# Flamingo block (two cross-attentions, two feed-forwards) on one core: the read-back of the probabilities, four orders behind other instructions, and the start of the projections

## The chip, the cores and the metric
One core of a Trainium2 chip. The metric is the device time of one execution in microseconds (us), as the median of several runs. Engines are named as the profile names them: PE (matmul), PEld (its weight loads), DVE (VectorE), ACT (ScalarE), POOL (GpSimd), SP (SyncE, which here only issues DMAs; its queue is "SPq").

## What is computed
Eight rows of 128 tokens, width 512, pass four steps, each added to the running `x` with a tanh gate. The first cross-attention has 32 heads of 128 and fills most of the time:

```
x = x + tanh(g_xattn[0]) * L0_xattn(layernorm(x), ctx)   # 32 heads, position bias, masked softmax
x = x + tanh(g_ffn[0])   * L0_ffn(layernorm(x))          # 4-bit weights, 512 -> 512
x = x + tanh(g_xattn[1]) * L1_xattn(layernorm(x), ctx)   # one head of width 512
x = x + tanh(g_ffn[1])   * L1_ffn(layernorm(x))          # base layer, router, 8 low-rank experts

# L0_xattn:  q = rms(x) @ w_q.T ; k = ctx @ w_k.T ; v = ctx @ w_v.T
#            p = softmax(mask(q k^T + position_bias)) ; out = x + (p v) @ w_out.T
```

## The kernel before
Every f32 product is made of three matmuls (L175 to L177): an operand is split into a high part (an fp32r cast on ACT, L166) and a low part (the difference, on DVE or POOL, L167), and high x high, high x low and low x high are added in PSUM. A 128x512 matmul follows its predecessor by about 0.227 us when nothing is late.

**Projections (0 to about 330 us).** `keys_and_queries` walks a list of 32 entries: 14 key pairs (a pair is two heads), 16 query pairs, the last 2 key pairs. The first two (`project_plainly`) use plain blocks: the inner halves in the outer loop, the four results copied by ACT (L552) after all matmuls. From the third on, `seven` uses seven half-size products P1 to P7 in the order P1, P5, P6, P2, P7, P4, P3. It has two PSUM accumulators that are read in between: `c1` is copied by ACT after P1 (L240), P6 (L247), P7 (L256) and P4 (L262), and the next product may add to it only after that copy; `c3` takes P5, is added by DVE to the copy of P7 (L257), and only then takes P3, after which DVE adds once more (L266). L251 adds P2. P4 and P3 of one entry run among the products of the next, so an iteration is some 9.5 us. Its weights are loaded two entries ahead (`load_pair`, L279); `sums_of` (L297 to L299, DVE) makes the sums of the entry after next at the end of each iteration, and `pair_parts` splits the parts in the next. The right operands come from the context (`context_operands`: eight blocks `cxB` split first, then four differences by DVE, L458, and their splits `cxT`) and from the rows of x (`query_operands`: for each of four steps two rows are normalised by `normed`, transposed by PE and split). `residual` (L577 to L583) scales rows of x, at entries 14, 16, 18 and 20. `early` is a generator of some 28 steps that prepares later weights (a load, a cast on ACT, a difference on POOL or DVE, two stores to DRAM; the last steps unpack the 4-bit weights: L841, L850, L851); it is pulled once or twice per entry from entry 13 on.

**Units (about 330 to 790 us).** 64 units, each one head for four rows. `unit(u)`: project_out of an earlier pair, some value products (`make_values`), `attend(u-4)`, `add_masks` (POOL, L633), `scores`: PE (L645), DVE adds the mask (L646) and takes the maximum (L650), DVE transposes the probabilities of u-3 (L691), ACT exponentiates (L660), DVE makes the factors (L665, L666), POOL multiplies (L668). `store_probs(u)` sends the tile to DRAM (L676); the loads for the next units are put behind that store on SP (L569 q and k, L363 bias, L279 weights); `move_probs(u)` reads it back in 32-row blocks with four DMAs (L683) into `moved`, of which there are two buffers. So the buffer that the read-back of u fills comes free when DVE has transposed u-2, which happens in unit u+1.

**End (about 790 us on).** `ending` interleaves the last units with the four-step tail (`ffn0`, `xattn1`, `ffn1`, a software pipeline over the eight rows; PE's order there and in the projections is fixed by `in_order`). The weights of the first feed-forward, `wf`, two DMAs of 1 MB, are issued ahead of it (L1031), as are four rows of biases (L1016); two of these are scaled by DVE (L1038, L1039).

**What sets the order.** Apart from the fixed orders on PE, the order of each engine's queue is settled when the program is built, by a list scheduler that goes by program order as priority and by its own estimate of durations. `behind(name)` adds an order only: on the engine of the marked instruction, what the block issues stands after it. Each queue then runs strictly in its order, so an instruction that waits holds up all behind it.

Of the kernel before, what the change touches and what calls it, by code (L numbers as in the profile page):

```python
# [14 lines left out]
ALU = mybir.AluOpType  # L15
# [48 lines left out]
def kernel(  # L64
# [55 lines left out]
    def wide_row(tag, name, dtype=F32):  # L120
        return slot([P, D], tag, name, dtype)
# [86 lines left out]
    def seven(name, left, right, kept, done, tokens=None):  # L208


        shape = [P, HALF * P] if tokens is None else [P, 2, N]

        def times(out, which, start, stop):
            w, t = left[which], right[RIGHT[which]]
            if tokens is None:
                terms = [
                    (
                        (w[:, 0, bass.ts(dc, P)], w[:, 1, bass.ts(dc, P)]),
                        (t[:, 0, dc, :], t[:, 1, dc, :]),
                    )  # L220
                    for dc in range(HK)
                ]
                product(out, terms, start, stop, skip_group_check=True)
                return
            for j in range(2):
                cols = bass.ts(2 * tokens + j, P)
                terms = [
                    (
                        (t[:, 0, dc, cols], t[:, 1, dc, cols]),
                        (w[:, 0, bass.ts(dc, N)], w[:, 1, bass.ts(dc, N)]),  # L230
                    )
                    for dc in range(HK)
                ]

                product(out[:, j, :], terms, start and j == 0, stop, skip_group_check=True)

        c1 = ptile(shape, "mm", f"c1_{name}")
        times(c1, "P1", True, False)
        c11 = kept(0, 0)
        mark("copy", nc.scalar.copy(c11, c1))  # L240
        yield
        c3 = ptile(shape, "av", f"c3_{name}")
        times(c3, "P5", True, False)
        yield
        times(c1, "P6", False, False)
        c12 = kept(0, 1)
        mark("copy", nc.scalar.copy(c12, c1))  # L247
        yield
        c2 = ptile(shape, "sc", f"c2_{name}")
        times(c2, "P2", True, True)  # L250
        mark("add", nc.vector.tensor_tensor(c11, c2, c11, ALU.add))  # L251
        done(0, 0, c11)
        yield
        times(c1, "P7", False, False)
        c22 = kept(1, 1)
        mark("copy", nc.scalar.copy(c22, c1))  # L256
        nc.vector.tensor_tensor(c22, c3, c22, ALU.add)  # L257
        done(1, 1, c22)
        yield
        times(c1, "P4", False, True)  # L260
        c21 = kept(1, 0)
        mark("copy", nc.scalar.copy(c21, c1))  # L262
        done(1, 0, c21)
        yield
        times(c3, "P3", False, True)
        nc.vector.tensor_tensor(c12, c3, c12, ALU.add)  # L266
        done(0, 1, c12)
        yield
# [147 lines left out]

    stats = keep([P, NB, 8], "stats")

    def normed(b):


        nc.vector.bn_stats(stats[:, b, 2:8], xs[b])
        nc.vector.bn_aggr(stats[:, b, 0:2], stats[:, b, 2:8])
        mean, var, r12 = (stats[:, b, i : i + 1] for i in range(3))
        nc.gpsimd.tensor_scalar(r12, var, 1.0 + 1e-5, 1e-10, ALU.mult, ALU.add)
        rsqrt(r12, r12)
        xq_b = wide_row("wo", f"xq_{b}")
        nc.vector.scalar_tensor_tensor(xq_b, xs[b], mean, lnw, ALU.subtract, ALU.mult)
        mark("xq", nc.scalar.activation(xq_b, xq_b, AF.Copy, scale=r12))
        return xq_b  # L430

    def right_pages(name):
# [2 lines left out]
    def context_operands():  # L435

        ops = right_pages("cx")
        ops["B12"] = page([P, 2, HK, HALF * P], "cxB12")
        blocks = {
            n: [cx_raw.pop((half, 2 * inner + i)) for i in range(HK)]  # L440
            for n, half, inner in (("B11", 0, 0), ("B12", 1, 0), ("B21", 0, 1), ("B22", 1, 1))
        }

        def put(n, i, src):
            o = ops[n]
            by_pool = i == 0 and n != "B11"
            split(o[:, 0, i, :], o[:, 1, i, :], src, nc.gpsimd if by_pool else nc.vector)

        for n, pair in blocks.items():
            for i, t in enumerate(pair):  # L450
                put(n, i, t)
        yield ops
        b11, b12, b21, b22 = blocks.values()
        for n, dst, one, two in (
            ("T1", b11, b12, b11), ("T2", b11, b22, b11), ("T3", b12, b22, b12), ("T4", b21, b21, b11)
        ):
            for i in range(HK):
                nc.vector.tensor_tensor(dst[i], one[i], two[i], ALU.subtract)  # L458
                put(n, i, dst[i])
        yield ops  # L460

    def query_operands():

        ops = right_pages("xq")
        for j in range(HALF):
            rows = [normed(j), normed(j + HALF)]
            blocks = []
# [37 lines left out]
            yield  # L507
            put("T3", t3)
            put("T4", t4)
            yield ops  # L510

    stored = {
# [19 lines left out]
    def project_plainly(kind, p, left, right):  # L532

        banks = {}
        for inner in range(2):
            for half in range(2):
                for i in range(2):
                    if inner == 0:
                        tag = ("mm", "av")[half]
                        banks[i, half] = ptile([P, HALF * P], tag, f"c{i}{half}_{kind[0]}{p}")  # L540
                    w, t = left[i], right[f"B{inner + 1}{half + 1}"]
                    terms = [
                        (
                            tuple(part[:, bass.ts(2 * inner + dc, P)] for part in w),
                            (t[:, 0, dc, :], t[:, 1, dc, :]),
                        )
                        for dc in range(HK)
                    ]
                    product(banks[i, half], terms, inner == 0, inner == 1)
        for (i, half), c in banks.items():  # L550
            t = slot([P, HALF * P], "kq", f"{kind}{i}{half}_{p}")
            mark("copy", nc.scalar.copy(t, c))  # L552
            nc.sync.dma_start(out=stored[kind, p][:, 2 * i + half], in_=t)

    fetched = {}

# [122 lines left out]
    def move_probs(u):  # L679
        moved = slot([P, NQ, HALF, Q32], "moved", f"moved_{u}")  # L680
        blocks = probs[u].rearrange("(i q) n f -> n q i f", q=Q32)
        for j in range(NQ):
            nc.sync.dma_start(  # L683
                out=moved[bass.ts(j, Q32)].rearrange("p i b k -> p i (b k)"), in_=blocks[j]
            )
        probs[u] = moved

    def transpose_probs(u):
# [199 lines left out]
    def keys_and_queries():  # L888
        nonlocal left, sums, before
        for n, (kind, p) in enumerate(order[:-1]):  # L890
# [24 lines left out]
                    else:  # L915
                        load_quad(0)
            before = now
            sums = sums_of(n + 2)
            if n == 3:
                with later():  # L920
                    prep_mask()
# [2 lines left out]
            if n in (14, 16, 18, 20):  # L924
                with later():
                    residual((n - 14) // 2)
            if n >= BEFORE - 1:
                for _ in range(2 - n % 2):
                    next(extra, None)
        for u in range(FIRST):  # L930
# [48 lines left out]
    def unit(u):  # L979
        p, r = divmod(u, 4)  # L980

        n = 2 * (u - OUT_LAG)

        goal = 14 + int(1.74 * (u - 3)) if u > 3 else 0
        if n >= 0:
            project_out(*divmod(n, NB))
        make_values((made + goal + 1) // 2)
        if u >= LAG:
            attend(u - LAG)
        if n >= 0:  # L990
            project_out(*divmod(n + 1, NB))
        make_values(goal)
        s = add_masks(u)
        for _ in range({0: 2, 1: 2, 2: 1, 3: 1, 4: 1}.get(u, 0)):
            next(last_keys)
        scores(u, s)
        store_probs(u)
        with behind("through"):
            loads(u + 1)
        move_probs(u)  # L1000
        if r in (2, 3):
            with behind("exp"):
                split_wo(2 * p + r - 2)
# [274 lines left out]
        nc.sync.dma_start(out=out[b], in_=o)  # L1278
        yield

    w_ffn = sum((load_page(f"wf{i}", ffn_kept[i]) for i in range(2)), [])
    wq1_p, bw, lora = [], {}, []
    rb = keep([P, NR], "rb")
    onehot = slot([P, NE * RANK], "bias", "onehot")[:NR]
# [24 lines left out]
    def ending():  # L1309

        outs = iter(range(2 * (NU - OUT_LAG), NP * NB))

        def project(n):
            for _ in range(n):
                project_out(*divmod(next(outs), NB))

        project(2)
        attend(NU - 4)
        with behind("x"):
            transpose_probs(NU - 3)  # L1320
        project(2)
        attend(NU - 3)
        project(1)
        yield
        project(3)
        with behind("x"):
            transpose_probs(NU - 2)
        make_values(14 * (H // 4 + 1) - 3)
        attend(NU - 2)
        yield  # L1330
        make_values(14 * (H // 4 + 1))
        transpose_probs(NU - 1)
        yield
        attend(NU - 1)
        project(4)
        yield
# [82 lines left out]
```

## Time and profile before

| | us |
|---|---|
| median of 3 runs (951.42 to 957.57) | 954.54 |
| the profiled execution, own time | 948.85 |
| its span, first to last instruction | 947.0 |
| PE busy / DVE / ACT / POOL | 918.2 / 667.2 / 504.9 / 468.2 |
| PE not busy over the span | 28.8 |
| of it in 0 to 24 / 24 to 56 / 155 to 310 | 4.4 / 3.9 / 5.7 |
| of it in 310 to 392 / 392 to 780 / 780 to 947 | 7.0 / 0.2 / 7.6 |

The profile numbers lines of the kernel (L257 is line 257). "PE x <- DVE y L257: 3.1, 2, 1.8" in the list of waits means that PE stood still before instructions on x until DVE's line 257 had written y: 3.1 us in all, 2 times, 1.8 us the longest. In the timeline a row gives start, duration, engine, line, operation and tiles, and in brackets the idle time before it and what ended that.

### The profile page before, as it was taken

The page shows a single profiled execution, that of the slowest core. Times are in us where ns is not written, and L with a number is a line of the kernel's source. Part 1 is how long each engine was busy: PE and PEld are TensorE (multiplying, and loading weights), DVE is VectorE, ACT ScalarE, POOL GpSimd, SP SyncE. Part 2 cuts the span into 40 slices and gives each one's busy share as a digit, 9 for nine tenths or more (in the row PEclk, how much of TensorE's full clock was granted, in tenths as well). Part 3 has the DMA queues.
Part 4 walks back from the last instruction along what each step waited for, and adds up shares of the span by engine and source line. Part 5 has one row for each costly group of instructions (what it writes and reads, how often), then busy time and mean ns, then how long its engine had stood idle before and what let it go on. Part 6 is the DMA issues. An engine that isn't in the chain of part 4 may idle for free.

```text
span 947.0 us, 16520 instructions
## 1 busy us (share of the span) xinstructions
PE 918.2 (97%) x5458; PEld 805.7 (85%) x5458; DVE 667.2 (70%) x1346; ACT 504.9 (53%) x1432; POOL 468.2 (49%) x516
## 2 busy tenths in 40 slices
PE   8999999999999989999999999999999999999998
PEld 6778888788877888899999999999999997888897
DVE  7787775677768786677667677667677676465686
ACT  5565654556564445454445545345454544487861
POOL 4744440113341365493865748476594852184441
PEclk9999999999999999999999999999999999999999
DMA  8545465698876946747676666868567556522001
GB/s 281 191 150 169 147 195 176 202 314 290 269 239 220 300 156 175 207 141 230 186 207 175 195 189 174 233 168 232 162 181 219 160 160 201 222 88 95 1 24 67
DMA packets 123908, 174.99 MB, mean 185 GB/s; under 512 B 16942, under 2 KB 52782, under 8 KB 122670
## 3 DMA queue, kind: packets, MB, share of 16 engines
q1 hardware_dynamic: 123822, 173.93, 60.5%
q8 instruction: 43, 0.70, 0.3%
q14 instruction: 43, 0.35, 0.1%
HBM read 109.85 MB, written 64.03 MB: 184 GB/s over the span
## 4 chain that ended last, share of the span: by engine, by line
PE 50%; DMA 3%; POOL 3%; ACT 3%; DVE 2%; issue 1%; SPq 1%; POOLq 0%; DVEq 0%; ACTq 0%
PE pso L175 6%; PE pso L177 6%; PE pso L176 6%; PE av L706 5%; PE c_v L175 5%; PE c_v L177 5%; PE c_v L176 5%; PE sc L645 5%; DMA k<-keys 1%; PE o L175 1%; DMA raw_wv<-in_wv_dram 1%; POOL cols L409 1%; PE o L177 1%; PE o L176 1%; ACT h L1068 1%
## 5 line engine op out<-in xcount | busy, mean ns | idle before, releaser
L660 ACT ACTIVATE s<-s,nm 128x128 f32<-128x128 f32 x256 | 99.8, 392 | 79.7 <-DVE nm L650 52.6
L725 DVE SCALAR_TENSOR_TENSOR x<-pso,tg,x 128x512 f32<-128x512 f32 x128 | 93.9, 742 | 34.0 <-PE pso L177 33.1
L175 PE MATMUL pso<-wo_h,a 128*128 128x512 f32 x256 | 106.0, 416 | 1.7 <-DVE x L725 1.7
L633 POOL TENSOR_TENSOR s<-mneg,bias 128x512 f32<-128x512 bf16 x64 | 75.7, 1190 | 59.7 <-DMA moved<-through 22.5
L668 POOL TENSOR_TENSOR s<-s,rs 128x512 f32<-128x512 f32 x64 | 66.7, 1041 | 69.1 <-DVE rs L666 51.3
L176 PE MATMUL pso<-wo_l,a 128*128 128x512 f32 x256 | 100.7, 395 | 0.0
L177 PE MATMUL pso<-wo_h,a 128*128 128x512 f32 x256 | 99.8, 399 | 0.0
L707 ACT CAST a<-av 128x512 fp32r<-128x512 f32 x64 | 37.3, 585 | 98.6 <-PE av L706 91.1
L175 PE MATMUL c_v<-wvP,cxT 128*128 128x256 f32 x288 | 84.2, 292 | 4.2 <-DVE keys L266 2.6
L176 PE MATMUL c_v<-wvP,cxT 128*128 128x256 f32 x288 | 82.9, 288 | 0.0
L177 PE MATMUL c_v<-wvP,cxT 128*128 128x256 f32 x288 | 82.3, 286 | 0.0
L706 PE MATMUL av<-pT,v 128*128 128x128 f32 x512 | 69.6, 277 | 0.0
L646 DVE TENSOR_TENSOR s<-sc,s 128x512 f32<-128x512 f32 x64 | 43.7, 685 | 34.3 <-POOL s L633 24.2
L645 PE MATMUL sc<-k,q 128*128 128x128 f32 x464 | 65.0, 275 | 1.6 <-DMA k<-keys 1.4
L706 PEld LDWEIGHTS av<-pT,v 128*128 128x128 f32 x512 | 65.2, 194 | 1.4
L645 PEld LDWEIGHTS sc<-k,q 128*128 128x128 f32 x464 | 60.8, 191 | 4.7 <-issue 1.9
L175 PE MATMUL c_v<-wvP,cxB 128*128 128x256 f32 x216 | 62.3, 288 | 2.1 <-DVE s L646 2.1
L708 DVE TENSOR_TENSOR a<-av,a 128x512 fp32r<-128x512 f32 x64 | 43.4, 679 | 28.9 <-ACT a L707 28.7
L177 PE MATMUL c_v<-wvP,cxB 128*128 128x256 f32 x216 | 61.9, 287 | 0.0
L175 PEld LDWEIGHTS c_v<-wvP,cxT 128*128 128x128 f32 x288 | 55.2, 192 | 7.8 <-DVE keys L266 2.8
L176 PE MATMUL c_v<-wvP,cxB 128*128 128x256 f32 x216 | 61.5, 285 | 0.0
L167 POOL TENSOR_TENSOR wvP<-raw_wv,wvP 128x512 fp32r<-128x512 f32 x41 | 53.6, 1317 | 7.8 <-ACT wvP L166 7.8
(280 smaller groups left out, 2809.7 us busy)
## 6 DMA issues: line engine op xcount, KB each, us to landing
keys<-keys SPq DMA_DIRECT2D x64, 256.0 KB, 3.1
queries<-queries SPq DMA_DIRECT2D x64, 256.0 KB, 3.8
through<-s SPq DMA_DIRECT2D x64, 256.0 KB, 2.5
moved<-through SPq DMA_DIRECT2D x256, 64.0 KB, 3.3
q<-queries SPq DMA_DIRECT2D x58, 256.0 KB, 4.2
k<-keys SPq DMA_DIRECT2D x58, 256.0 KB, 4.7
raw_wk<-in_wk_dram SPq DMA_DIRECT2D x32, 256.0 KB, 4.0
raw_wq<-in_wq_dram SPq DMA_DIRECT2D x32, 256.0 KB, 3.9
```

The lines of the kernel that those rows point to most:

```text
L167: mark("low", (low_engine or nc.vector).tensor_tensor(low, src, wide(high), ALU.subtract))
L175: nc.tensor.matmul(out, lhsT=lh, rhs=rh, start=first, stop=False, **more)
L176: nc.tensor.matmul(out, lhsT=lh, rhs=rl, start=False, stop=False, **more)
L177: nc.tensor.matmul(out, lhsT=ll, rhs=rh, start=False, stop=last, **more)
L633: nc.gpsimd.tensor_tensor(s, mneg[:, half], bias.unsqueeze(2).to_broadcast([P, NQ, HALF, Q32]), ALU.add)
L645: nc.tensor.matmul(ps[:, j, :], lhsT=q[:, cols], rhs=k[:, cols], start=True, stop=True)
L646: nc.vector.tensor_tensor(s, by_block(ps), s, ALU.add)
L660: e = nc.scalar.activation(one, one, AF.Exp, bias=nm[:, j : j + 1], accum_out=sm[:, j : j + 1])
L668: mark(f"norm{u}", nc.gpsimd.tensor_tensor(s, s, factors, ALU.mult))
L706: nc.tensor.matmul(av[:, b, :], lhsT=v[:, cols], rhs=pT[:, b, :], start=True, stop=True)
L708: mark("al", nc.vector.tensor_tensor(al, av, wide(ah), ALU.subtract))
L725: "x", nc.vector.scalar_tensor_tensor(xs[b], ps, factor, xs[b], ALU.mult, ALU.add, **out)
```

## The change
1. `sums_of` at the end of an iteration is put behind the DVE addition L257, which now carries the mark "add". (The mark also serves `later()`, so `residual`, `early` and the mask preparation stand behind L257 where they stood behind L251.)
2. `normed`: the statistics move to `row_stats`, called one step ahead, with one more small DVE instruction (minus mean times factor); the row is scaled first, by ACT out of x, and DVE multiplies by the weight after it. Before, DVE subtracted and multiplied and ACT scaled last.
3. `context_operands`: the low parts of the first eight blocks all go to DVE (three went to POOL); the differences and later low parts stand behind the last of them.
4. `project_plainly`: the second pair finishes one result after the other, and each result is copied and stored as soon as it is complete.
5. `early` starts at entry 11 and not 13.
6. `move_probs(u)` is issued in unit u+1, after the loads and behind the store of u+1 (the last two: before the last store, and at the start of `ending`).
7. The two loads of `wf` move into `ending`, behind the last read-back.

```diff
-        nc.vector.tensor_tensor(c22, c3, c22, ALU.add)
+        mark("add", nc.vector.tensor_tensor(c22, c3, c22, ALU.add))
...
+        nc.vector.scalar_tensor_tensor(
+            stats[:, b, 5:6], mean, -1.0, r12, ALU.mult, ALU.mult
+        )
+
+    def normed(b):
         xq_b = wide_row("wo", f"xq_{b}")
-        nc.vector.scalar_tensor_tensor(xq_b, xs[b], mean, lnw, ALU.subtract, ALU.mult)
-        mark("xq", nc.scalar.activation(xq_b, xq_b, AF.Copy, scale=r12))
+        nc.scalar.activation(
+            xq_b, xs[b], AF.Identity, bias=stats[:, b, 5:6], scale=stats[:, b, 2:3]
+        )
+        nc.vector.tensor_tensor(xq_b, xq_b, lnw, ALU.mult)
...
-        def put(n, i, src):
+        def put(n, i, src, engine=nc.vector):
             o = ops[n]
-            by_pool = i == 0 and n != "B11"
-            split(o[:, 0, i, :], o[:, 1, i, :], src, nc.gpsimd if by_pool else nc.vector)
+            nc.scalar.copy(o[:, 0, i, :], src)
+            mark(
+                "low",
+                engine.tensor_tensor(o[:, 1, i, :], src, wide(o[:, 0, i, :]), ALU.subtract),
+            )
...
+        marks["lows"] = marks["low"]
...
-                nc.vector.tensor_tensor(dst[i], one[i], two[i], ALU.subtract)
-                put(n, i, dst[i])
+                with behind("lows"):
+                    nc.vector.tensor_tensor(dst[i], one[i], two[i], ALU.subtract)
+                    put(n, i, dst[i], (nc.gpsimd, nc.vector)[i])
...
+        row_stats(0)
+        row_stats(HALF)
         for j in range(HALF):
             rows = [normed(j), normed(j + HALF)]
...
+            if j + 1 < HALF:
+                row_stats(j + 1)
+                row_stats(j + 1 + HALF)
             yield ops
...
+        turns = [(inner, half, i) for inner in range(2) for half in range(2) for i in range(2)]
+        if p:
+            turns.sort(key=lambda turn: (turn[1], turn[2], turn[0]))
+        for inner, half, i in turns:
...
+            product(banks[i, half], terms, inner == 0, inner == 1)
+            if inner:
+                t = slot([P, HALF * P], "kq", f"{kind}{i}{half}_{p}")
+                mark("copy", nc.scalar.copy(t, banks[i, half]))
+                nc.sync.dma_start(out=stored[kind, p][:, 2 * i + half], in_=t)
...
-            sums = sums_of(n + 2)
+            with behind("add"):
+                sums = sums_of(n + 2)
...
-            if n >= BEFORE - 1:
+            if n >= BEFORE - 3:
                 for _ in range(2 - n % 2):
                     next(extra, None)
...
         scores(u, s)
+        if u == NU - 1:
+            move_probs(u - 1)
         store_probs(u)
         with behind("through"):
             loads(u + 1)
-        move_probs(u)
+            if 0 < u < NU - 1:
+                move_probs(u - 1)
...
-    w_ffn = sum((load_page(f"wf{i}", ffn_kept[i]) for i in range(2)), [])
+    w_ffn = []
...
+        move_probs(NU - 1)
+        with behind("moved"):
+            for i in range(2):
+                w_ffn.extend(load_page(f"wf{i}", ffn_kept[i]))
         project(2)
         attend(NU - 4)
```

## The prediction
> **What bounds the kernel now.** The page comes first: which engine is full. Then a table of windows (time, busy time per engine, granted clock, DMA share, GB/s) shows where PE is not.
>
> ```profile
> PE 918.2 (97%) x5458; PEld 805.7 (85%) x5458; DVE 667.2 (70%) x1346; ACT 504.9 (53%) x1432; POOL 468.2 (49%) x516
> ```
> ```profile
> 24.00:56.00 32.00, 28.12 (x125) 22.04 (x124) 26.39 (x64) 19.85 (x50) 23.71 (x36) 1.00 0.49 159
> ...
> 310.00:345.00 35.00, 31.48 (x180) 27.83 (x179) 27.17 (x40) 14.99 (x37) 16.73 (x12) 0.95 0.79 267
> ...
> 392.00:780.00 388.00, 387.85 (x2681) 358.14 (x2680) 273.16 (x478) 187.44 (x617) 252.87 (x218) 1.00 0.67 188
> ```
> PE bounds it. From 392 to 780 us it never stands still, so nothing can be won there and much lost. The 28.8 us in which PE is not busy lie in the projections, the entry into the units and the end; whoever shortens no wait of PE there gains nothing. So next the list of what PE waited for (total, times, longest):
>
> ```profile
> PE c_q L175 <- DVE queries L257: 3.1, 2, 1.8
> PE c_q L175 <- ACT queries L240: 2.6, 2, 1.6
> PE c_v L175 <- DVE keys L266: 2.6, 1, 2.6
> PE c_v L175 <- DVE s L646: 2.1, 1, 2.1
> PE c_k L176 <- DVE cxB L167: 1.7, 3, 1.3
> PE c_k L175 <- ACT keys L247: 1.7, 1, 1.7
> PE pso L175 <- DVE x L725: 1.7, 3, 1.0
> PE c_k L175 <- ACT keys L240: 1.6, 1, 1.6
> PE sc L645 <- DMA k<-keys: 1.4, 1, 1.4
> ```
> These are single events, and for each the timelines of DVE and ACT show the instruction in front of the late one. Two of DVE's rows:
>
> ```profile
> 274.22 0.43 DVE L297 TENSOR_TENSOR more_wq<-raw_wq 128x256 f32<-128x256 f32 x1 [3.37 <-DMA raw_wq<-in_wq_dram]
> ...
> 275.36 0.68 DVE L257 TENSOR_TENSOR queries<-c_q,queries 128x512 f32<-128x512 f32 x1
> ```
> L257's input was ready: ACT ended the copy L256 at 269.9. It stood behind a sum that waited 3.37 us for a weight.
>
> Around a wait more is lost than is listed: at 36.64 the first matmul lasts 0.50 us and not 0.39, and the next follows after 0.33 and not 0.23, some 0.2 to 0.3 us each time. And the granted clock is 0.95 and 0.96 in the windows from 310 and 345, which is 0.05 x 35 = 1.75 us and 0.04 x 47 = 1.9 us; each drop stands right behind a wait of over 2 us (DVE keys, DVE s).
>
> **The change part by part** (us of the profiled execution; gains negative)
>
> *Sums behind L257.* In front of the two P3 that waited 3.1, L257 can go at 271 and 293: all of it, -3.1. The sums wait for the same load as before, one instruction later (0.6); behind them stand low parts that PE needs an iteration later. At 166 and 187 PE waited 2.6 for copy L240: ACT had two residual rows in front (L583, 1.5 us), which waited for DVE's L581, which stood among the sums waiting for a load until 163.04. L581 now comes after L257 and the sums, at some 164.1, while L240's input is there at 162.8 (1.36 after L256, as at 63.42 and 64.78), so the scheduler should put the copy first. Of 2.6 I take -2.0; if it keeps the residual first, 0.
>
> *Plain pair finished one by one.* At 36.64 PE waited 1.6 for L240, behind four copies L552 issued from 31.52 to 35.51 with casts among them. Now three lie before 29. -1.6. The same matmuls and DMAs are issued. The low part that held PE 0.5 at 33.84 stood in the same jam: -0.3.
>
> *Rows scaled first.* The 1.7 for L247 at 52.21: ACT stood at L429 waiting for two DVE multiplications that took 2.06 together while POOL worked. ACT's first step now needs only statistics made long before. But DVE now waits for ACT ahead of its multiplication (0.68), and its additions stand behind that: -1.2 of 1.7. Eight more small DVE instructions (0.16, row L580) have cover in DVE's idle time, 32 less 26.4; uncovered, 1.3.
>
> *First low parts on DVE.* Three low parts leave POOL, where they took 5.12 together from 9.10, and cost DVE 3 x 0.69. PE's two waits there, 0.34 (POOL) and 1.27 (DVE, late at 11.30 behind two differences that took 2.39) go: -1.6. The differences start some 3 us later, but their products are only needed at 32.7. The earlier waits, 5.0 to 9.2, are for loads and stay. [...]
>
> *`early` two entries sooner.* Its work moves about 19 us forward (two iterations of 9.5); per step a load, a cast (0.62), a low part (POOL 1.3 to 1.5, DVE 0.69) and two stores of 0.4 on SP. At 330.97 two L841 took 2.96 on DVE, and L850 and a score addition stood in front of L266, for which PE waited 2.6; then 0.6 and 0.3 on ACT's list. These go, -3.2, with the clock drop behind them, -1.75. Entries 11 and 12 take three steps more: ACT is 55.89 of 99 busy in the window from 56 to 155, and that is the cover; if a store is late, loads queue behind it, and sums, now out of L257's way, are late.
>
> *Read-back a unit later.* 256 DMAs of 0.43 us on SP move behind a store and two to four loads of 0.43. SP loses its two waits there (54 for the store to land, 33 for the transposition), which held up the next store by up to 3.7; as PE waits for none of this between 392 and 780, that is worth 0 there. At the entry I take -1.6 of the 3.5 for L646 and for k, and a quarter of the second clock drop, -0.45: the bias load that made the first late (issued 365.56, 5.57 us) keeps its place behind the store. The price: the list for `moved` gives
>
> ```profile
> DMA to landing us min/median/max: 1.8/3.3/6.1
> ```
> Taking the times of before, I put each read-back of u behind the store and loads of unit u+1, added three issues and 3.4 us, and compared with the transposition of u. The slack falls from a median of 7.4 (least 0.5) to 2.0; 13 of 62 come late, 17.5 us in all, on DVE. Two rows say what that costs PE: at 388.86 DVE stood 1.99 for a read-back and PE lost nothing; at 791.56 it stood 3.29 and PE lost 0.47. So 0 to 17.5 x 0.47 / 3.29 = 2.5; I take 1.1, as most are under 2.
>
> *`wf` loads behind the last read-back.* Two DMAs of 1 MB move from 786 to some 800; they landed in 8.4 and are first used at 817: 8 us of cover. The bias row that held DVE 3.29 shared the queues with them. -0.8 of the 1.7 for L725.
>
> *Waits that take their place.* Every queue is sorted anew. Between nothing and a wait for each one removed, I put two of the mean size in the list, 2.0: +4.0.
>
> Sum: 3.1 + 2.0 + 1.6 + 0.3 + 1.2 + 1.6 + 3.2 + 1.75 + 1.6 + 0.45 + 0.8 = 17.6; the restarts of some ten waits at 0.2 add 2.0: 19.6 gained. Given back 1.1 + 4.0 = 5.1. Net -14.5: 948.85 - 14.5 = 934.35 for such an execution. It lay 5.7 under the median of the runs, which I keep: 954.54 - 14.5 = 940.0.
>
> The clock by the page's rule (the Trainium skill, TensorE: Matmul & The Clock Gate, HAM clock gate): half rate after a whole idle window of about 3.4 us. Here waits of 2.6 and 2.1 were enough, while three of 1.6 to 1.7 before 56 us were not. If by the rule these drops had another cause and stayed, the net would be 14.5 - 2.2 = 12.3.
>
> **The rivals**
>
> *Given back at the entry* (0.28). The projections win, but the re-sorted entry and end keep waits as large as before: 3.2 + 1.75 + 1.6 + 0.45 + 0.8 = 7.8 fall away, net -6.7 or, with one more wait, -4.7: about 949. For it: those waits come from ACT, POOL and DMA together, and POOL idles 5.2 us for a load that doesn't move. Against: DVE's and POOL's `early` work is visibly in front.
>
> *The read-back too late: slower* (0.12). If it lands not in 3.4 but in 6.1 us, as it now queues behind q, k and weights of 256 KB, 41 of 62 come late, 82 us on DVE. DVE runs in order, and the x additions that free PE's banks stand behind. It decides from about a quarter of that on PE: 0.25 x 82 = 20.5 eats the 19.6. Half of it gives -14.5 + 41 = 26.5, or 981; a third, 967. For it: a slack of 2.0. Against: DVE is idle 115 of 388 us, and 1.99 cost nothing.
>
> *The change does not do what it says* (0.05). The scheduler had statistics and sums early already and moves them as before: 954 or so.
>
> *As summed* (0.55): 940, own range 930 to 946.
>
> **How the numbers follow.** A measurement of this kernel tells about 1%, 9.5 us, from no change: faster ends at 945. Of the likeliest, 0.48 of 0.55 lies under 945; of the rival at 949, 0.08. Faster 0.57 (with a little for more than I count). Slower takes the late read-back, 0.12 and 0.01; the rest, 0.30, is the same. The range goes from 929, nothing given back and the untaken rest of each part too (0.6 for L240, 0.5 for L247, 1.9 for L646 and k, 1.4 of clock, 0.9 for L725: 19.6 + 5.3 = 24.9), to 957, a read-back that eats the gain; the slower rival beyond is left out.
>
> **What would show it.** Right: no PE wait for L257, for keys L240 or L247, for cxB beyond 10 us; DVE's L297 after L257; the granted clock 1.00 from 310 to 392; SP without waits at L683. Wrong: DVE idle before L691 with "DMA moved" of over 40 us; PE waits between 392 and 780; the residual still ahead of L240; a clock drop elsewhere.

## The result and the profile after

The changed kernel took 942.62 us (median of 4 runs, 938.8 to 943.57) beside 952.98 for the kernel before (951.3 to 957.57): ratio 0.9876, 95% interval 0.9829 to 0.9923. Once more on another chip, where the kernel before took 948.41, it was 937.96 (experiment e9): ratio 0.9891 (0.9873 to 0.9910). By the medians both are 10.4 us faster; by the ratio the first is 11.8, with an interval from 7.3 to 16.3. The forecast was 14.5. The two executions with a profile differ less: span 947.0 before, 941.4 after, because the one of before lay under its median and the one of after did not.

The windows of the kernel after (columns: window, its length, busy us of PE, PEld, DVE, ACT and POOL with instruction counts, granted clock, DMA share, GB/s):

```profile
24.00:56.00 32.00, 28.73 (x127) 22.53 (x126) 29.67 (x70) 21.85 (x52) 24.08 (x37) 1.00 0.54 165
310.00:345.00 35.00, 33.51 (x227) 30.68 (x226) 25.32 (x43) 18.39 (x46) 11.51 (x10) 1.00 0.58 203
345.00:392.00 47.00, 41.22 (x287) 37.74 (x286) 27.23 (x51) 21.74 (x77) 24.86 (x22) 0.98 0.69 191
392.00:780.00 388.00, 385.65 (x2641) 355.49 (x2641) 268.94 (x477) 187.52 (x621) 251.63 (x216) 0.99 0.69 186
```

From 310 to 345 us the clock is 1.00 and PE is busy 2.0 us more than before. From 24 to 56 it is busy 0.6 more, and DVE is now busy 29.67 of 32. From 392 to 780 PE stands still for 2.35 us, where it was 0.15 before; all of it is one wait at 774.95. From 345 to 392 it stands still for 5.8 us, before for 3.5.

Its list of what PE waited for (total, times, longest):

```profile
PE av L726 <- DVE pT L711: 3.7, 3, 2.5
PE sc L664 <- DMA k<-keys: 2.3, 1, 2.3
PE c_k L177 <- DVE wkP L167: 1.9, 2, 1.1
PE c_q L175 <- ACT queries L247: 1.6, 3, 0.5
PE c_v L175 <- ACT wvP L166: 1.5, 1, 1.5
PE c_v L175 <- DVE s L665: 1.4, 1, 1.4
```

(Lines have moved: the transposition L691 is L711, the score addition L646 is L665, the score matmul L645 is L664, the read-back L683 is L702, the residual L583 is L602.) The waits for L257, L266, queries L240 and x L725 are gone. Those for the transposition and for k are new or larger, and they are the two largest. DVE's rows for the part that was read from 274.22 on before:

```profile
266.95 0.68 DVE L257 TENSOR_TENSOR queries<-c_q,queries 128x512 f32<-128x512 f32 x1
267.55 0.41 DVE L297 TENSOR_TENSOR more_wq<-raw_wq 128x256 f32<-128x256 f32 x1
```

The addition goes first and the sum follows. The read-back has become late as forecast; the first line is DVE's wait for it (2.0 before), the second the time from issue to landing (1.8/3.3/6.1 before):

```profile
DVE pT L711 <- DMA moved<-through: 17.8, 8, 4.3
```
```profile
DMA to landing us min/median/max: 1.8/4.4/7.8
```

These are the two places where PE stood for longest, one for the transposition and one for k:

```profile
390.00 2.00 PE L726 MATMUL av<-pT,v 128*128 128x128 f32 x8 [2.47 <-DVE pT L711]
...
774.95 1.32 PE L664 MATMUL sc<-k,q 128*128 128x128 f32 x8 [2.35 <-DMA k<-keys]
```

The wait at 390.00 is read backwards through DVE, POOL and SP (timelines of each, in order of time):

```profile
377.26 0.71 DVE L711 STREAM_TRANSPOSE pT<-moved 128x512 f32<-128x512 f32 x1 [4.27 <-DMA moved<-through]
```
```profile
378.69 1.04 POOL L687 TENSOR_TENSOR s<-s,rs 128x512 f32<-128x512 f32 x1 [4.44 <-DVE rs L685]
```
```profile
379.75 0.34 SPq L695 DMA_DIRECT2D through<-s  x1
380.13 0.43 SPq L588 DMA_DIRECT2D q<-queries  x1
380.67 0.40 SPq L588 DMA_DIRECT2D k<-keys  x1
381.11 0.43 SPq L363 DMA_DIRECT2D bias<-in_pbias_dram  x1
```
```profile
386.62 2.29 POOL L652 TENSOR_TENSOR s<-mneg,bias 128x512 f32<-128x512 bf16 x2 [3.32 <-DMA bias<-in_pbias_dram]
```
```profile
387.82 0.69 DVE L665 TENSOR_TENSOR s<-sc,s 128x512 f32<-128x512 f32 x1 [4.45 <-POOL s L652]
```

A read-back held DVE for 4.27; behind the transposition stood the factors `rs`, for which POOL waited to multiply; behind that the store of the next unit; behind the store, on SP, the bias load; and for the bias POOL and then DVE stood again, ahead of the transposition that PE needed. With the read-back as before (e10) the same store goes out at 376.73 and the same bias load at 378.11, 3.0 sooner.

After both waits of PE, the matmuls on 512 columns follow one another by 0.43 us in place of 0.23: the trace records the clock at 0.5 for 3.413 us from 390.0 and from 775.8.

### The profile page after: what moved, and what is told of

It is laid out like the page before. It is cut to its first block, busy times and chain, and to the rows that moved or that the text cites. A ratio compares the mean times of both kernels' runs of the same rounds, so it can differ in the third digit from the quotient of the medians.

```text
span 941.4 us, 16540 instructions
## 1 busy us (share of the span) xinstructions
PE 917.7 (97%) x5458; PEld 805.3 (86%) x5458; DVE 673.1 (72%) x1357; ACT 506.4 (54%) x1432; POOL 462.4 (49%) x513
## 4 chain that ended last, share of the span: by engine, by line
PE 72%; DMA 9%; DVE 6%; POOL 5%; ACT 4%; issue 2%; SPq 2%; DVEq 0%; POOLq 0%; ACTq 0%
PE pso L177 5%; PE pso L175 5%; PE pso L176 5%; PE c_v L175 5%; PE av L726 5%; PE c_v L176 5%; PE c_v L177 5%; PE sc L664 5%; PE c_k L177 4%; PE c_k L175 4%; PE c_q L175 4%; PE c_k L176 4%; PE c_q L176 4%; PE c_q L177 4%; DMA moved<-through 4%
## 5 line engine op out<-in xcount | busy, mean ns | idle before, releaser
L664 PE MATMUL sc<-k,q 128*128 128x128 f32 x464 | 64.6, 275 | 2.5 <-DMA k<-keys 2.3
L664 PEld LDWEIGHTS sc<-k,q 128*128 128x128 f32 x464 | 60.4, 191 | 5.9 <-issue 2.9
L665 DVE TENSOR_TENSOR s<-sc,s 128x512 f32<-128x512 f32 x64 | 43.8, 685 | 25.8 <-POOL s L652 16.3
L177 PEld LDWEIGHTS pso<-wo_h,a 128*128 128x128 f32 x256 | 48.6, 190 | 12.4 <-DVE a L728 2.0
```

The source lines that it names most:

```text
L177: nc.tensor.matmul(out, lhsT=ll, rhs=rh, start=False, stop=last, **more)
L664: nc.tensor.matmul(ps[:, j, :], lhsT=q[:, cols], rhs=k[:, cols], start=True, stop=True)
L665: nc.vector.tensor_tensor(s, by_block(ps), s, ALU.add)
```

## The experiments

The theory after the result: the orders in the projections gave what was forecast or more, and the later read-back took part of it back. The rival: the start of the projections fell short, and the read-back costs nothing but DVE's idle time. "Us" from a ratio below is (1 - ratio) times the kernel before of the same run: 952.81 us for e1 to e4, 948.15 for e5 to e8, 948.41 for e9 to e12.

**e1, the change without the later read-back**

```diff
-        if u == NU - 1:
-            move_probs(u - 1)
         store_probs(u)
         with behind("through"):
             loads(u + 1)
-            if 0 < u < NU - 1:
-                move_probs(u - 1)
+        move_probs(u)
...
-        move_probs(NU - 1)
         with behind("moved"):
```

> The changed kernel, but each unit's read-back is issued in its own unit again (the last loads of wf still stand behind the last read-back). My theory, that the later read-back costs what was lost at 361 to 393 us and at 775 us (3.1 and some 3 us by the milestones of PE): DVE waits for a read-back fall from 17.8 us to under 4, the wait of 2.3 us for k at 775 and the clock drop behind it go, and the kernel is 3 to 6 us faster than the changed one, 937 to 940. Rival, that the entry and the end lose as much without it, as in the kernel before (5.6 us at 373 to 388): the same as the changed kernel, 941 to 944. Rival, that the earlier issue holds up the stores behind it and the loads behind those: slower than the changed kernel, 946 or more.

936.03 us (934.28 to 938.62), ratio 0.9831 (0.9808 to 0.9853): 6.6 under the changed kernel's 942.62. DVE waits for the read-back 0.9 us, once, and it lands sooner (the same two lines as above, the wait and the landing):

```profile
DVE pT L711 <- DMA moved<-through: 0.9, 1, 0.9
```
```profile
DMA to landing us min/median/max: 1.7/3.2/6.3
```

No clock drop lies in this execution. The signs of the theory came, and the gain is a little over its 3 to 6. By the ratios it is only 4.3, and the two intervals overlap; e9 and e10 below compare the same two kernels on one chip.

**e2, the kernel before with the later read-back alone** (the same lines, put into the kernel before)

> The kernel before with only the read-back a unit later (wf stays where it was). My theory: DVE waits for read-backs rise from 2 us to 15 or more, PE loses some of that at the entry and at the end, and it is 2 to 6 us slower than the kernel before. Rival, that the freed SP queue brings loads and stores earlier: 2 to 5 us faster. Rival, that it makes no difference: within 2 us.

958.82 us (954.32 to 963.34), ratio 1.0057 (1.0038 to 1.0075): slower by 5.4. DVE's wait and the landing are those of the changed kernel, and PE waits for the transposition:

```profile
DVE pT L691 <- DMA moved<-through: 17.6, 9, 4.1
```
```profile
DMA to landing us min/median/max: 1.8/4.4/9.9
```
```profile
PE av L706 <- DVE pT L691: 4.2, 5, 2.6
```

Part of the profiled loss has nothing to do with the read-back (a wait of 2.4 for wkP at 45 us, before any unit runs); from the entry to the end the execution, the slowest of its eight, loses some 9 us.

**e3, the later read-back ahead of the loads, still behind the store**

```diff
         with behind("through"):
-            loads(u + 1)
             if 0 < u < NU - 1:
                 move_probs(u - 1)
+            loads(u + 1)
```

> The changed kernel with the read-back still a unit later and behind the store, but ahead of the loads and not after them. If what makes it late is that it queues behind 0.5 to 0.8 MB of loads (landing 4.4 us in the median, 3.3 before), it lands in 3.3 to 3.8 again and starts 1.3 us sooner: DVE waits for it fall under 8 us, and the kernel gains 1 to 4 us on the changed one. If it is late because the store it stands behind is late, little changes: within 1 us. Rival: q and k, now 1.75 us later, hold PE in its place: slower by 2 us or more.

940.88 us (940.12 to 942.66), ratio 0.9882 (0.9864 to 0.9900): 4.9 above e1 and 1.7 under the first run of the changed kernel (by the ratios level with it). The read-back is in time; the k load, now four issues later, is not:

```profile
DVE pT L711 <- DMA moved<-through: 3.5, 3, 1.8
```
```profile
DMA to landing us min/median/max: 1.9/2.5/5.7
```
```profile
PE sc L664 <- DMA k<-keys: 6.6, 5, 2.7
```

So here the place in SP's queue behind the store is paid for by one of the two, and no gain from choosing which is shown.

**e4, the sums behind L257 alone** (part 1, in the kernel before)

> The kernel before with only the sums (and the residual and early work that goes by the same mark) behind the last addition. My theory: PE's two waits for L257 (3.1 us with 0.3 each for the restart, 3.7) go, the two for L240 (2.6, with restart 3.1) turn into three for L247 of 0.5, so that some 4.5 us are won by the end of the query pairs, and 3 to 6 us in all. Rival, that the sums are only late one step further on, and low parts hold PE instead: under 1.5 us.

944.22 us (940.3 to 946.1), ratio 0.9909 (0.9879 to 0.9939): 8.7 faster by the ratio, 6.2 by the span (940.9), which is over the 3 to 6 expected. It is the largest single part. The query pairs no longer wait for L257 and L240; three waits of 0.52 for L247 take the place of the two for L240. Compared matmul by matmul with the kernel before, PE gains 4.6 us over the first 15 query pairs, close to the 4.5 expected. The rest comes from outside them: the wait for L266 at the entry is gone too, and one of 1.9 for L257 on the values and one of 2.3 for x have come.

**e5, the start alone** (parts 2, 3 and 4, in the kernel before)

> The kernel before with parts 2, 3 and 4 alone (rows scaled first, first low parts on VectorE, plain pair finished one by one). The prediction's terms for these were 1.6 + 1.9 + 1.2 and about 1.0 of restarts: 5.7 us, ratio 0.994. The rival from the trace after: the first low parts give their 2.5, but VectorE's statistics of all eight rows still run at 17 to 26 us, so the waits from 31 to 52 us stay (4.4 in place of 5.0): some 3 us in all, ratio 0.997. Waits of TensorE for cxB of 10 us and later gone under both; under the first no wait for wkP, keys L240 or L247 between 30 and 53 us, under the second over 3 us of them.

946.36 us (943.85 to 948.94), ratio 0.9974 (0.9958 to 0.9990): 2.5 faster. The fifth entry ends at 63.71 in place of 65.94, 2.2 sooner, although the first plain pair alone is already 2.5 sooner. From 31 to 53 us

```profile
PE c_k L177 <- DVE wkP L167: 1.8, 2, 1.2
...
PE c_k L175 <- ACT keys L240: 0.7, 1, 0.7
```

are left, with a clock drop behind them at 36.2 (3.413 us at half the rate, 1.7). The measured 2.5 lies just under the second expectation, some 3, and well under the first. In the nine other traces with these three parts, none with a drop between 31 and 65 us, the fifth entry ends 2.5 to 3.2 sooner than before.

**e6, `early` two entries sooner alone** (part 5, in the kernel before: `BEFORE - 3` for `BEFORE - 1`)

> The kernel before with part 5 alone (later weights prepared from entry 11 on). The prediction gave it 3.2 us of waits and 1.75 us of clock, 5 us, ratio 0.995, with the wait for keys L266 gone and the granted clock 1.00 from 310 to 345 us. The rival: VectorE's and ScalarE's lists are only sorted anew, the wait for L266 is replaced by others of its size before 392 us, and the time stays within 2 us of before.

947.17 us (942.65 to 949.81), ratio 0.9979 (0.9957 to 1.0001): 2.0, not certain. The signs came out: no wait for L266, clock 1.00 from 310 to 345. But with the sums still ahead of L257, the projections lose some of it again before the entry (at the 16th query pair PE is 2.0 later than before, a third wait for L240, a new one for L247):

```profile
PE c_q L175 <- ACT queries L240: 4.6, 3, 2.0
...
PE c_q L175 <- ACT queries L247: 1.2, 1, 1.2
```

**e7, e1 with `early` as before**

> The changed kernel with the read-back as before (the best version so far, 936.0 in its run) and the later weights prepared from entry 13 on, as before. If starting two entries sooner is worth what the prediction gave it, 5 us come back: about 941, with a wait of over 2 us for keys L266 and a clock below 1.00 between 310 and 345. If the sums behind the last addition were already enough to keep VectorE free there, it stays at 936 to 937 and L266 is not waited for.

940.83 us (939.89 to 944.42), ratio 0.9929 (0.9904 to 0.9955), beside 0.9867 (0.9844 to 0.9890) for the same kernel with `early` sooner (e10): 5.9 come back. The size is that of the prediction, 5; the named wait isn't. L266 stays away, and these stand in its place, with clock drops at 340.4 and 391.6:

```profile
PE pso L175 <- DVE x L745: 3.2, 2, 2.3
PE c_v L175 <- DVE s L665: 2.4, 1, 2.4
PE c_v L175 <- DVE v L257: 1.9, 1, 1.9
```

So part 5 is worth 2.0 alone and 5.9 in company. That it needs part 1, to keep the sums out of L257's way, is what e6's waits suggest; no run has these two parts alone.

**e8, e1 with the residual's rows one by one**

```diff
-            if n in (14, 16, 18, 20):
+            if 14 <= n < 22:
                 with later():
-                    residual((n - 14) // 2)
+                    residual(n - 14)
```

`residual(b)` scales one row, and makes the factors of a pair of rows only where b is even. ACT's rows in the changed kernel, ahead of the first wait for L247, and then in e8:

```profile
164.04 1.52 ACT L602 ACTIVATE x<-x,stats 128x512 f32<-128x512 f32 x2 [2.73 <-DVE stats L600]
165.47 0.56 ACT L262 COPY queries<-c_q 128x512 f32<-128x512 f32 x1
165.93 0.40 ACT L166 CAST wqP<-more_wq 128x256 fp32r<-128x256 f32 x1
166.24 0.58 ACT L247 COPY queries<-c_q 128x512 f32<-128x512 f32 x1
```
```profile
164.48 0.82 ACT L606 ACTIVATE x<-x,stats 128x512 f32<-128x512 f32 x1 [2.73 <-DVE stats L600]
165.20 0.57 ACT L262 COPY queries<-c_q 128x512 f32<-128x512 f32 x1
165.67 0.41 ACT L166 CAST wqP<-more_wq 128x256 fp32r<-128x256 f32 x1
165.97 0.58 ACT L247 COPY queries<-c_q 128x512 f32<-128x512 f32 x1
```

> The changed kernel with the read-back as before, and the residual's two rows of one step scaled in two entries, one each (entries 14 to 21), in place of two in entries 14, 16, 18 and 20. Theory: each of the four waits for L247 of 0.5 us near 167, 187, 207 and 226 us came from two residual instructions of 0.76 in front of L262 and L247 on ScalarE; one of 0.76 leaves room. 4 x (0.5 + 0.2 of restart) = 2.8 us less than that version: 933 to 934. Rival: one of 0.76 is still too much, eight smaller waits take the place of four, and the time stays at 936.

934.01 us (932.27 to 934.36), ratio 0.9844 (0.9824 to 0.9864). L247 comes 0.27 sooner while PE, by its first query pair, is 0.44 later than in the changed kernel: 0.71 of room where 0.5 was missing. From 155 to 310 us PE no longer stands still.

```profile
155.00:310.00 155.00, 155.00 (x684) 127.75 (x683) 132.56 (x272) 92.56 (x224) 45.02 (x35) 1.00 0.81 268
```

Whether the whole is better than e1 only a run on the same chip tells, so the last four ran together.

**e9, the changed kernel; e10, e1 again; e11, e8 again; e12, e11 with the bias load a unit earlier**

```diff
-        if r == 3:
+        if r == 2:
             load_bias(p + 1)
```

> The changed kernel itself once more, on one chip with the next three, because the time of the kernel before differs by some 5 us between the chips of the earlier runs (952.8 and 948.15). Theory (the later read-back costs about 6 us): it stays 5 to 8 us above the version with the read-back as before. Rival: most of that difference was between chips, and the two lie within 3 us.

> The changed kernel with the read-back as before, as in e1, once more. Theory: 934 to 937, 5 to 8 us under the changed kernel in this run; rival: within 3 us of it.

> As e8 (read-back as before, the residual's two rows in two entries), once more beside e10. The trace of e8 had no wait of TensorE from 56 to 310 us, and 2.8 us were expected of that, of which a late k load took 1.2 and a clock drop back. Theory: 1 to 3 us less than e10. Rival: the waits only move to the entry, and it is equal to e10.

> As e11, with the bias load of the next head pair issued one unit earlier. Theory: at the entry GpSimd stood 4.2 us for the bias load (issued 351.96, used at 356.5) and TensorE 1.1 to 1.5 for the score addition behind it; that wait falls away, 1.3 with restart: 1 to 2 us less than e11. Rival: the maximum or the k load is late next, or the earlier load delays q and k behind it on the queue, and the time is the same or up to 1 us more.

| kernel, one chip, 5 rounds | us (lowest to highest) | ratio to before (95%) |
|---|---|---|
| e9 changed | 937.96 (937.12 to 938.28) | 0.9891 (0.9873 to 0.9910) |
| e10 read-back as before | 935.09 (934.54 to 937.37) | 0.9867 (0.9844 to 0.9890) |
| e11 and residual in single rows | 932.55 (931.93 to 934.76) | 0.9841 (0.9818 to 0.9863) |
| e12 and bias a unit earlier | 929.11 (928.90 to 929.68) | 0.9801 (0.9781 to 0.9821) |

The read-back costs 2.9 here (2.3 by the ratios), and 6.6 (4.3) by e1. The theory of e9 and e10, 5 to 8, failed, and the rival, within 3 us, came out, if barely. The traces show that what differs is less the waits than the clock. The changed kernel's first trace is 6.7 us longer than e1's and holds two drops, 3.4 us together, where e1's has none; e9's is 2.3 longer than e10's and holds one drop, where e10's has two. Without the drops 3.3 and 4.0 us are left. In e9 a wait of 1.91 at the same place had no drop, while in e10 a k wait of 2.10 had one (the last section shows why):

```profile
388.66 1.13 PE L726 MATMUL av<-pT,v 128*128 128x128 f32 x8 [1.91 <-DVE pT L711]
```
```profile
373.02 1.13 PE L664 MATMUL sc<-k,q 128*128 128x128 f32 x8 [2.10 <-DMA k<-keys]
```

e11 gained 2.5 on e10, as expected. e12 gained 3.4 more, above its expectation. The fourth and fifth mask additions on POOL, in e11 and then in e12:

```profile
356.28 2.29 POOL L656 TENSOR_TENSOR s<-mneg,bias 128x512 f32<-128x512 bf16 x2 [3.99 <-DMA bias<-in_pbias_dram]
```
```profile
349.46 1.17 POOL L656 TENSOR_TENSOR s<-mneg,bias 128x512 f32<-128x512 bf16 x1
...
352.85 1.17 POOL L656 TENSOR_TENSOR s<-mneg,bias 128x512 f32<-128x512 bf16 x1
```

The eighth and ninth, which use the next bias load, move as well (380.42 in e11, 373.99 and 377.36 in e12), so two waits went and not one. In e12 no wait of PE is longer than 1.4 us, none is for `s`, and from 345 to 392 it is busy 46.36 of 47 at a clock of 1.00 (before: 43.53, 0.96):

```profile
345.00:392.00 47.00, 46.36 (x333) 43.13 (x332) 32.11 (x60) 23.14 (x78) 30.00 (x27) 1.00 0.72 212
```

e12 is the fastest version: 2.0% under the kernel before and 0.9% under the change. A third buffer for `moved`, which would let the early read-back start without waiting for the transposition, was not tried.

## Why the prediction was right, and where its terms were not

| part | forecast, with restarts | alone or undone, by ratio (us) |
|---|---|---|
| 1, sums behind L257 | -5.9 | -8.7 (e4; by the span -6.2) |
| 2, 3, 4, the start | -5.7 | -2.5 (e5) |
| 5, `early` sooner | -5.2 | -2.0 (e6), -5.9 with the rest (e7 beside e10) |
| 6, read-back later | -0.95 | +2.3 (e9, e10), +4.3 (e1), +5.4 (e2); by medians +2.9, +6.6, +6.0 |
| 7, `wf` later | -0.8 | no run |
| waits that take their place | +4.0 | +3.1 (by the list of waits, see below) |

**Sums: right in cause, and near in size.** The two P3 go at once, and copy L240 now runs ahead of the residual, as forecast. What the prediction did not name is that the residual then stands in front of the next copies, L262 and L247: 1.6 us in the list above, gone in e8. The ratio gives more than the span because the profiled execution of before lay under its median. By the span the size is right to 0.3, but that is partly chance: over the query pairs, where the waits lay, PE gained 4.6 of the 5.9 (e4). With the residual in single rows (e8) it gains 6.6 there.

**The start: the first waits right, the rest mis-sized, and the terms not additive.** The waits at 10.9 and 13.1 are gone, and the first pair ends 2.5 us sooner (28.65 for 31.16). From 31 to 53 us PE lost 4.97 us at waits before (its matmuls' starts against their usual spacing) and 4.38 after (1.13 and 1.34 for wkP, 0.70 for L240, 1.21 for L247), where 3.1 were to go (plain pair 1.6, low part 0.3, rows 1.2). Nor does the gain of the first pair last. In the ten traces with these three parts it ends anywhere from 28.64 to 32.15 us, and yet the fifth entry always ends from 62.73 to 63.71, 2.2 to 3.2 sooner than before: a pair that ends sooner waits longer behind it.

The step that failed is "cover in DVE's idle time, 32 less 26.4". The three low parts push the differences behind them into this window, and the eight small instructions come on top: 2.1 + 1.3 = 3.4, beside a growth from 26.39 to 29.67 = 3.3. With 2.3 us left the cover was nearly used up, and wkP, which two matmuls wait for, comes from DVE. The rows of the kernel after, DVE and then PE, show what stood in front of the second of them:

```profile
32.54 1.27 DVE L436 TENSOR_TENSOR xq<-xq,lnw 128x512 f32<-128x512 f32 x2
34.27 0.16 DVE L427 SCALAR_TENSOR_TENSOR stats<-stats 128x1 f32<-128x1 f32 x1 [0.45 <-POOL stats L409]
34.35 0.42 DVE L309 TENSOR_TENSOR more_wk<-raw_wk,more_wk 128x256 f32<-128x256 f32 x1
34.68 0.42 DVE L167 TENSOR_TENSOR wkP<-more_wk,wkP 128x256 fp32r<-128x256 f32 x1
```
```profile
35.15 0.50 PE L177 MATMUL c_k<-cxT,wkP 128*128 128x512 f32 x1 [1.06 <-DVE wkP L167]
```

ACT had ended the cast for this low part at 31.4. It stood behind the two multiplications by the weight (L436) and one of the new small instructions (L427), both from part 2. The forecast priced the eight small ones by their length, 0.16; three of them also waited for POOL's statistics, 2.1 us together. On ACT two rows of part 2 (L433, 1.52 us from 29.61) stood in front of the last copy of the plain pair, which came at 32.25; three copies had been forecast before 29, and two came. How much of the 1.2, 1.6 and 1.9 of parts 2, 3 and 4 each one lost wasn't separated.

**`early`: right in size, with the reason half told.** The L266 wait went, and the clock is 1.00 from 310 to 345. e7 shows that without this part other waits, of 1.9, 2.4 and 2.3, stand there, and e6 that alone it gives back more than half.

**The read-back: the lateness right, its price on PE too low.** DVE waited 17.8 us; 17.5 had been worked out, in 8 waits rather than 13. Two steps failed. First, the conversion to PE: 17.5 x 0.47 / 3.29, taken from one row at the end of the program and cut to 1.1. That row, L1039 at 791.56, waited for a bias row (`bb`) and not for a read-back. A transposition that waits holds up the factors behind it, these the store, and the store everything on SP behind it, the next read-back among it; the chain to 390.00 above shows one round of that. Where the wait falls decides its price: five of the eight, 7.9 us together from 547 to 767 us, cost PE nothing, while those of 4.27 and 3.36 at the entry and the end stand beside PE's two longest waits. The prediction named the x additions as what stands behind, and not the factors. Second, that POOL's bias load "keeps its place behind the store" was taken as no change, though the store itself comes later. The landing, too, was taken at 3.4, the median of before, while each read-back now follows two to four loads of 128 or 256 KB: 4.4 was measured. This part should stand in the sum with +2 to +6 and not with -0.95. The start was counted some 3 too high and the sums up to 3 too low. So it is partly luck that the total came within some 4 us: errors of about 3 us and more lie on both sides of the sum. The slower rival was right in kind: its waits came, at 2 to 7 us and not at the 41 that it priced.

**`wf` behind the last read-back.** Its 0.8 is not shown. The waits for x near 788 and 792 are gone in the changed kernel, but not by this move: e1, e8, e10 and e11 have it too, and there PE waits 0.9 to 1.0 us for x at that place (before: 1.0 and 0.5). The second of the two is gone in e4, e5 and e6 as well, which lack the move. What goes with the move is DVE's wait for the bias row: 2.6 to 3.3 us without it (before, e4, e5, e6), 0.2 to 0.4 in those four runs. No run undid this part alone.

**Waits that take their place.** L247 for queries (1.6) and wvP (1.5 at 314.93) are 3.1 of the 4.0; the k wait of 2.35 at 774.95 comes on top and belongs to the read-back: all four kernels with the later read-back have it, at 1.1 to 2.35 (after, e9, e2, e3), while e1 has 0.4 there and e10 none.

**The clock.** The two drops of before went with the waits in front of them, as the rows said. Two others came behind new waits, at 390.0 and 775.8: the sign "a clock drop elsewhere", which gives back the 1.75 and 0.45 counted as gain. The prediction's "three of 1.6 to 1.7 before 56 us" misreads its list: two are single waits, the third (cxB) is a sum of three, the longest 1.3. The rival "given back at the entry" asked for 949, and its bias wait did stay, but the projections' gain was too large for it: the parts alone add up to -8.7 - 2.5 - 2.0 + 5.4 = -7.8, and `early` in company makes it about -11.7.

## What to carry to other kernels

Before an instruction that waits for a DMA on an in-order engine, put whatever is ready and has a waiting consumer; then look for the next instruction that stands in front of the same consumer, since here the wait moved to the next one (from the sum to the residual). A transfer that is moved behind others on one queue is to be priced with its new neighbours and with the consumer's stage where it has the least slack, not with the median of before; where one of the two had to be late here, changing their order showed no gain (e3). Cover on an engine is spent once: add up what all parts of a change put on it in one window.

## What the runs showed of the hardware

Between the first and the last matmul the 14 traces hold 22 drops of the clock, each 3.41 us long at 0.50, 1.7 us lost at most. Of 21 gaps of 2.3 us and more between the starts of two matmuls, 15 had a drop begin in them or within 2 us behind; of 29 gaps between 1.7 and 2.3, five; two more drops came behind several shorter waits in a row. A gap of 2.00 had one (e4, 36.9) and one of 2.89 had none (e2, 408.6). So a wait of 2 to 3 us costs itself and, more often than not from 2.3 on, 1.7 more, and two executions of one kernel differ by that: the changed kernel's spans of 941.4 and 936.3 hold two drops and one.

The traces tell more than the length of a gap does. In each of them all changes of the clock lie on one grid of 3.413 us, to within 2 ns. Add up PE's idle time in each step of that grid (of every gap over 0.4 us between the starts of two matmuls, what exceeds 0.227). A drop follows each of the 22 steps with 1.93 us or more, and none of the other 3748 steps at full clock, which have at most 1.92; counting shorter gaps too blurs this border by 0.1 us. So a gap costs a drop if enough of it falls into one step: of e10's gap of 2.38, 2.15 did; e9's 2.18 was split into 1.02 and 0.94, and of e2's 2.89 at most 1.86 fell into one.

The Trainium skill (TensorE: Matmul & The Clock Gate, HAM clock gate) gives a free-running window of 3413 ns, which is the measured length and the measured grid, and the grid explains that equal gaps differ. It asks for at least one idle window of about 3.4 us before the clock falls; no gap here reached that (the longest is 3.12 us), 1.93 us of idle time in one step was enough, and the measured drops decide.
